# Two counts of a routing block in one PSUM bank

## The chip, the core and the metric

The kernel runs on one core of a Trainium2 chip. A core has a matrix engine (TensorE, PE in the profile; its weight loads are shown apart as PEld), a vector engine (VectorE, DVE), a scalar engine (ScalarE, ACT), a general engine (GpSimd, POOL) and a queue that mostly starts DMA transfers (SyncE, SP). Each engine takes its instructions in the order in which the program was built, and waits at an instruction until what it needs is there. Matrix products land in PSUM, which has eight banks of 2 KB per partition, 512 fp32 numbers each. The metric is the time of one execution on the device in microseconds, lower is better.

## What is computed

There are 8192 tokens of width 512. Each is normalised (layernorm); the result is the token plus an attention by random features plus a mixture of 64 experts plus a shared expert. Cut to what matters here:

```python
xn = _layernorm(x, axis=-1)
# attention: features of the tokens times features of the weights
feats = 1 / sqrt(512) * AB * exp(xn @ (ab[:, None] * proj).T - 0.5 * sum(xn * xn) * ab * ab)
attn = feats @ weights.T
# routing
scores = sigmoid(tokens @ router_w)                    # 64 experts
# the 4 best of 8 groups of experts, then the 8 best experts in them
topk_w, topk_idx = top_k(masked_scores, 8)
topk_w = topk_w / sum(topk_w) * 2.5
pos = number of earlier (token, slot) pairs that chose the same expert   # cumsum of a one-hot
valid = pos < 256                                      # capacity of an expert
# each expert: its tokens, silu(g) * u, down; added back with its weight
# shared expert: silu(tokens @ sg) * (tokens @ su) @ sd
out = x + attn + routed + shared
```

For the capacity the kernel has to know, per expert, how many tokens chose it up to each token. Those running counts are what the change touches.

## The kernel before, in words

The tokens are cut into 16 blocks of 512 (NB, TB), and each block into four parts of 128 tokens (NS). Products with fp32 accuracy are made of three matmuls on rounded upper parts and remainders (`products`, L108). The routing logits have such parts too, but the router's two parts lie side by side in one weight tile, so eight matmuls of 512 columns make them (L364).

The first stage, about the first 405 us, goes over the blocks with two strands. `dense` does an even block's shared expert (tiles ps_gu, then ps_o) and its attention features (ps_f, L501 to L507) and output (ps_o, L511). `routing(step)` is called after every step of `dense` and moves the routing of the blocks on by one step each; five steps make a block (GAP), so two blocks are routed while one even block is worked through densely. The features and outputs of most odd blocks are done later, in pieces between the experts' work. In the second stage the experts follow one another, each with two gathers of its rows by POOL, gate, up and down products, and a scatter that adds to the output.

The steps of one block's routing are the generator `look_up(b)`:

- `normalize`, ahead of it, writes the normalised tokens xw by ScalarE (L301). From block 5 on a DMA started by ScalarE copies them to a tile xc (L314), so that they can be read in another number type.
- `turn` transposes the block on TensorE into four PSUM tiles ps_x (L331), taken in turn from the pools `ps_tr` and `ps_sm`; ScalarE (L98) and VectorE (L101) split each into xT_h and xT_l.
- The logits: eight matmuls into ps_l (L364), copied by ScalarE to lt (L374).
- Four transposes bring lt back into token order, ps_lt (L381); ScalarE copies one half (L388), VectorE adds the other (L389), ScalarE writes exponentials into xw (L391).
- VectorE ranks the groups and takes the best eight (L397 to L426), makes the mask of chosen experts mask_r (L428) and prior_r, the number of earlier choices in the same partition (L435).
- One idle step. In it the next block's `turn` is issued, because the next block starts five steps after this one.
- The counts: one matmul of 256 columns into ps_b (L443), the counts before each part, and four of 128 columns into ps_u (L454), the running counts. ScalarE copies ps_u to cu (L462), which a DMA writes to the table upto in device memory (L463).
- In the next step VectorE reads ps_b twice to update the tables begun (L482), which later tell where each expert's tokens begin.

The blocks are called in order, so in one routing step the counts of block b come first and the logits of block b + 1 second; one step later begun of block b comes first and ps_lt of block b + 1 second.

PSUM is divided by pools: two banks for `ps_tr`, four for `ps_mm` (all products of `dense`), two for `ps_sm`:

```python
ps_tr = ctx.enter_context(tc.tile_pool(name="ps_tr", bufs=2, space=PSUM))
ps_mm = ctx.enter_context(tc.tile_pool(name="ps_mm", bufs=4, space=PSUM))
ps_sm = ctx.enter_context(tc.tile_pool(name="ps_sm", bufs=2, space=PSUM))
```

Half of the transposes, ps_l, ps_lt, ps_b and ps_u all share the two banks of `ps_sm`. Which tile gets which bank, and in what order an engine's instructions stand, is decided by a scheduler as the program is built. It keeps the given priorities, lets an instruction go ahead when it thinks its bank and operands are free, and adds the waits that order the engines, for each bank of PSUM too. `behind(a, b)` only adds that a stands behind b. So a change of the tiles can change the order of instructions, even though none is added.

Of the kernel before, what the change touches and what calls it, by code (L numbers as in the profile page):

```python
# [9 lines left out]
FP = mybir.dt.float32  # L10
# [8 lines left out]
P = 128  # L19
# [3 lines left out]
E = 64  # L23
# [8 lines left out]
TB = 512  # L32
NB = T // TB
NS = TB // P
# [19 lines left out]
def rfs_attention_moe_kernel(  # L54
# [22 lines left out]
    ps_sm = ctx.enter_context(tc.tile_pool(name="ps_sm", bufs=2, space=PSUM))  # L77
# [39 lines left out]
    def behind(a, b):  # L117

        tc.add_manual_dep(a.ins, b.ins.name, ORDER, reason="what a needs comes late")
# [223 lines left out]
    def look_up(b):  # L343
# [90 lines left out]
        for s in range(1, NS):  # L434
# [4 lines left out]
        yield  # L439
        yield  # L440

        pb = ps_sm.tile([P, NS, E], FP, tag="sm", name="ps_b")
        counted = nc.tensor.matmul(  # L443
            pb.rearrange("p s e -> p (s e)"),
            ones_r,
            prior_r.rearrange("p s e -> p (s e)"),
            start=True,
            stop=True,
        )
        behind(counted, last["pe"])  # L450
        pu = ps_sm.tile([P, NS // 2, P], FP, tag="sm", name="ps_u")
        for q in range(NS // 2):
            for part, (w, v) in enumerate(((mask_r, tri_r), (prior_r, ones_r))):
                nc.tensor.matmul(  # L454
# [197 lines left out]
    for rc in range(RC):  # L652
        pool, tag = ((ps_sm, "sm"), (ps_tr, "tr"))[rc // 2]
        ps_w.append(pool.tile([P, H], FP, tag=tag, name="ps_f"))
        projected(parts(wT, KC), rc, ps_w[rc])
    late = look_up(0)
    next(late)
    upper0 = last["upper"]
# [182 lines left out]
    def routing(t):  # L841

        for b in sorted(fronts):
            if next(fronts[b], fronts) is fronts:
                del fronts[b]
        b, k = divmod(t + GAP, GAP)
        if k == (b == 1) and b < NB:
            fronts[b] = look_up(b)
            next(fronts[b])
        if k == GAP - 3 and b + 1 < NB:  # L850
            normed[b + 1] = normalize(b + 1, *roots(b + 1, statistics(xbs[b + 1])))
        if k == 1 and b + 2 < NB:
            xbs[b + 2] = load_tokens(b + 2)
# [141 lines left out]
```

## Time and profile before

| what | value |
|---|---|
| three runs | 1320.38 us median (1320.17 to 1323.96) |
| the profiled execution | 1324.84 us, its span on the core 1323.1 us |
| granted TensorE clock | 0.998 |
| stage to 390 us: TensorE busy | 78.65 of 85.00 us, then 297.24 of 305.00 us |
| 390 to 445 us, where the experts begin | 51.68 of 55.00 us |
| 445 us to the end | 872.46 of 878.10 us |
| one count matmul, 256 columns, of ps_b | 0.28 us, the next starts 0.12 us later |
| one copy cu of ps_u by ScalarE | 0.37 us, 16 of them |
| one begun by VectorE | 0.48 us, 32 of them |
| one matmul of 512 columns | 0.39 us, the next starts 0.23 us later |

A row of the profile names the source line, engine and operation, the tile written and those read, the shapes and how many there are. A row of the timeline begins with the start and the time it took, and in brackets stands how long the engine was idle before it and what it waited for. Matmuls overlap, so a matmul's own time is longer than the distance between two starts. All is one execution.

### The profile page before, as it was taken

The numbers are of one execution on the slowest core, as the hardware profiler recorded it, in microseconds if no ns is written. First come the engines' busy times: TensorE is split into PE (matmuls) and PEld (weight loads), VectorE is DVE, ScalarE is ACT, GpSimd is POOL, SyncE is SP. The second block draws the span as 40 slices with busy tenths as digits, with TensorE's granted clock in tenths as the row PEclk, the third lists the DMA queues.
The fourth block names the chain that finished last, engine by engine and source line by source line (L and its number), as shares of the span: only waits on it lengthen the run. The fifth ranks groups of instructions, "written<-read, shape, count | busy, mean of one in ns | idle before, by whom it ended". The sixth has DMA issues, their size and how long they took to land.

```text
span 1323.1 us, 21351 instructions
## 1 busy us (share of the span) xinstructions
PE 1300.0 (98%) x7648; PEld 1138.6 (86%) x7648; DVE 929.2 (70%) x1922; ACT 646.1 (49%) x1017; POOL 573.1 (43%) x670
## 2 busy tenths in 40 slices
PE   8999999999999999999999999999999999999998
PEld 6888787788788899999999999999999999988886
DVE  7978768768765677777677767777776776643555
ACT  5644443444332455656556556655565565540111
POOL 3122012012105667778667676767677754210000
PEclk9999999999999999999999999999999999999999
DMA  7665675675585989999999999999999999875995
GB/s 253 239 229 198 234 259 197 233 266 209 193 314 178 305 216 306 270 276 271 317 271 264 309 265 283 248 294 285 266 259 303 281 259 234 227 220 178 317 319 191
DMA packets 192313, 338.60 MB, mean 256 GB/s; under 512 B 15952, under 2 KB 87632, under 8 KB 192208
## 3 DMA queue, kind: packets, MB, share of 16 engines
q1 hardware_dynamic: 153456, 245.93, 54.1%
q0 software_dynamic: 32768, 79.78, 27.3%
q10 hardware_dynamic: 5984, 11.54, 2.5%
q8 instruction: 60, 0.98, 0.3%
q14 instruction: 45, 0.37, 0.1%
HBM read 220.66 MB, written 104.99 MB: 246 GB/s over the span
## 4 chain that ended last, share of the span: by engine, by line
PE 90%; DVE 4%; DMA 4%; ACT 1%; issue 1%; POOL 0%; SPq 0%; DVEq 0%; ACTq 0%
PE ps_gu L108 41%; PE ps_o L108 14%; PE ps_e L108 13%; PE ps_fu L108 6%; PE ps_y L108 5%; PE ps_f L108 3%; PE ps_t L769 3%; DMA xc<-xw 2%; PE ps_l L364 2%; PE ps_x L331 2%; DMA xb<-in_L_attn_x_dram 1%; DVE f L491 0%; DVE r L499 0%; DVE fT L101 0%; DVE st L275 0%
## 5 line engine op out<-in xcount | busy, mean ns | idle before, releaser
L819 POOL DMA_INDIRECT out_dram<-ye,who x128 | 225.5, 1762 | 186.5 <-ACT ye L818 136.4
L108 PE MATMUL ps_gu<-gT,gu_h 128*128 128x256 f32 x2048 | 291.3, 284 | 0.0
L108 PEld LDWEIGHTS ps_gu<-gT,gu_h 128*128 128x128 f32 x2048 | 268.6, 192 | 5.3 <-ACT gu_h L98 1.0
L699 POOL DMA_INDIRECT at<-upto,line x128 | 140.2, 1095 | 80.1 <-DMA q<-norms 41.4
L108 PE MATMUL ps_gu<-gT,gu_l 128*128 128x256 f32 x1024 | 167.3, 286 | 0.2 <-DVE gu_l L101 0.2
L101 DVE TENSOR_TENSOR gu_l<-gu,gu_h 128x1024 fp32r<-128x1024 f32 x128 | 155.6, 1218 | 6.9 <-ACT gu_h L98 6.9
L752 POOL DMA_INDIRECT xg<-xnw,who x128 | 143.1, 1118 | 39.0 <-issue 32.6
L108 PE MATMUL ps_e<-d_h,ehT 128*128 128x512 f32 x512 | 148.6, 392 | 0.0
L108 PEld LDWEIGHTS ps_gu<-gT,gu_l 128*128 128x128 f32 x1024 | 140.9, 192 | 0.7 <-DVE gu_l L101 0.4
L98 ACT CAST gu_h<-gu 128x1024 fp32r<-128x1024 f32 x128 | 132.5, 1058 | 0.0
L246 POOL TENSOR_TENSOR a<-rstd,ve 128x4 f32<-128x4 f32 x45 | 10.5, 233 | 272.0 <-DVE rstd L242 269.6
L98 ACT CAST ehT<-sg 128x512 fp32r<-128x512 f32 x64 | 39.8, 621 | 156.6 <-DVE sg L499 153.7
L818 ACT ACTIVATE ye<-ps_e,we 128x512 f32<-128x512 f32 x128 | 88.6, 695 | 56.4 <-PE ps_e L108 55.6
L108 PEld LDWEIGHTS ps_e<-d_h,ehT 128*128 128x128 f32 x512 | 94.7, 188 | 18.8
L499 DVE SCALAR_TENSOR_TENSOR sg<-sg,ps_gu 128x512 f32<-128x512 f32 x64 | 44.0, 688 | 68.4 <-PE ps_gu L108 68.2
L101 DVE TENSOR_TENSOR d_l<-d,d_h 128x1024 fp32r<-128x1024 f32 x64 | 78.3, 1224 | 7.6 <-ACT d_h L98 7.2
L101 DVE TENSOR_TENSOR gT<-ps_t,gT 128x512 fp32r<-128x512 f32 x128 | 83.2, 682 | 0.0
L101 DVE TENSOR_TENSOR ehT<-sg,ehT 128x512 fp32r<-128x512 f32 x64 | 44.4, 694 | 51.8 <-ACT ehT L98 51.8
L505 ACT ACTIVATE f<-f,ab 128x512 f32<-128x512 f32 x64 | 46.4, 725 | 69.3 <-DVE f L491 69.3
L108 PE MATMUL ps_o<-fW_h,fT 128*128 128x512 f32 x288 | 79.3, 392 | 0.2 <-ACT fT L98 0.2
L108 PE MATMUL ps_e<-d_l,ehT 128*128 128x512 f32 x256 | 79.4, 391 | 0.0
L108 PE MATMUL ps_o<-d_h,hT 128*128 128x512 f32 x256 | 78.3, 396 | 0.0
(180 smaller groups left out, 2513.6 us busy)
## 6 DMA issues: line engine op xcount, KB each, us to landing
gu<-in_L_ffn_gate_w_dram SPq DMA_DIRECT2D x64, 512.0 KB
gu<-in_L_ffn_up_w_dram SPq DMA_DIRECT2D x64, 512.0 KB
d<-in_L_ffn_down_w_dram SPq DMA_DIRECT2D x64, 512.0 KB
xnw<-xw SPq DMA_DIRECT2D x32, 577.0 KB
xb<-in_L_attn_x_dram SPq DMA_DIRECT2D x32, 512.0 KB
out_dram<-xb SPq DMA_DIRECT2D x32, 512.0 KB
xT_h<-turned SPq DMA_DIRECT2D x30, 512.0 KB
xT_l<-turned SPq DMA_DIRECT2D x30, 512.0 KB
```

What stands on the lines that cost most here:

```text
L98: return nc.scalar.copy(dst, src)
L101: return on.tensor_tensor(dst, src, hi.bitcast(FP), ALU.subtract)
L108: last["pe"] = nc.tensor.matmul(ps, w[c][a], v[c][b], start=(start and part == 0 and c == 0), stop=(stop and part == 2 and c == n - 1),)
L331: last["turn"] = nc.tensor.transpose(pr[:, ts(s, P)], src(s)[:, ts(kc, P)], ident if dt is FP else ident_r)
L364: logits = nc.tensor.matmul(pl, rwp[:, kc].rearrange("p t e -> p (t e)"), v[kc], start=(n == 0 and kc == 0), stop=(n == 1 and kc == KC - 1),)
L499: nc.vector.scalar_tensor_tensor(dst, dst, 0.5, u, ALU.mult, ALU.mult)
L505: nc.scalar.activation(f, f, AF.Exp, scale=ab[:, rc : rc + 1])
L699: nc.gpsimd.indirect_dma_start(out=at[:, e % TE, h, :], out_offset=None, in_=upto, in_offset=bass.IndirectOffsetOnAxis(ap=line[:, e, h : h ...
L752: nc.gpsimd.indirect_dma_start(out=xgs[e][:, h, :], out_offset=None, in_=xnw, in_offset=bass.IndirectOffsetOnAxis(ap=who[:, e, h : h + 1], ...
L769: turned_s = nc.tensor.transpose(pr[:, c, ts(h, P)], xr[:, h, ts(c2 * 2 + c, P)], ident_r)
L818: nc.scalar.activation(ye[:, h, :], po, AF.Copy, scale=wes[e][:, h : h + 1])
L819: now = nc.gpsimd.indirect_dma_start(out=out, out_offset=bass.IndirectOffsetOnAxis(ap=who[:, e, h : h + 1], axis=0), in_=ye[:, h, :], in_o ...
```

## The change

The tiles ps_b and ps_u, which had a bank each, become the two halves of one tile ps_bu. The shapes and contents of the five count matmuls are as before, and so are the copies and the tables. The pool keeps its two banks.

```diff
@@ look_up @@
         yield
         yield
 
-        pb = ps_sm.tile([P, NS, E], FP, tag="sm", name="ps_b")
+
+        both = ps_sm.tile([P, 2, TB // 2], FP, tag="sm", name="ps_bu")
+        pb = both[:, 0].rearrange("p (s e) -> p s e", e=E)
         counted = nc.tensor.matmul(
-            pb.rearrange("p s e -> p (s e)"),
+            both[:, 0],
             ones_r,
             prior_r.rearrange("p s e -> p (s e)"),
             start=True,
             stop=True,
         )
         behind(counted, last["pe"])
-        pu = ps_sm.tile([P, NS // 2, P], FP, tag="sm", name="ps_u")
+        pu = both[:, 1].rearrange("p (q t) -> p q t", t=P)
         for q in range(NS // 2):
```

The lines behind it stand two lines lower in the changed kernel.

## The prediction

> **What bounds the kernel now.** I read the page's totals and its chain first, then the waits of TensorE, then the timeline around the instructions that the diff touches.
>
> ```profile
> span 1323.1 us, 21351 instructions
> PE 1300.0 (98%) x7648; PEld 1138.6 (86%) x7648; DVE 929.2 (70%) x1922; ACT 646.1 (49%) x1017; POOL 573.1 (43%) x670
> ...
> PE 90%; DVE 4%; DMA 4%; ACT 1%; issue 1%; POOL 0%; SPq 0%; DVEq 0%; ACTq 0%
> ```
>
> TensorE is busy 98% of the span, and 90% of the chain that ended last runs on it. So only what changes TensorE's own order or its pauses can move the end, and microsecond for microsecond, unless a later wait takes it back. Next, all waits of the logits matmuls (L364, tile ps_l), the instructions that are to get another bank:
>
> ```profile
> PE ps_l L364 <- ACT cu L462: 1.5, 7, 0.2
> PE ps_l L364 <- DVE xw L471: 1.2, 5, 0.2
> PEld ps_l L364 <- ACT cu L462: 4.5, 7, 0.6
> PEld ps_l L364 <- issue: 3.2, 5, 0.6
> ```
>
> Seven blocks' logits wait for ScalarE's copy cu (L462), five for something on VectorE. The timeline shows both kinds. First a block whose counts fall at the start of the features (columns: start, time, engine, line, what, how many, and the idle time before):
>
> ```profile
> 136.97 1.14 PE L108 MATMUL ps_f<-xT_h,pT_h 128*128 128x512 f32 x4
> 137.26 0.87 DVE L482 SCALAR_TENSOR_TENSOR begun<-ps_b,slot,begun 128x256 f32<-128x256 f32 x2
> 137.37 0.62 ACT L98 CAST hT<-r 128x512 fp32r<-128x512 f32 x1 [1.02 <-DVE r L499]
> 137.90 0.37 ACT L462 COPY cu<-ps_u 128x256 f32<-128x256 f32 x1
> 138.05 0.68 DVE L101 TENSOR_TENSOR hT<-r,hT 128x512 fp32r<-128x512 f32 x1
> ...
> 138.32 1.21 PE L364 MATMUL ps_l<-xT_h,rwp 128*128 128x512 f32 x4 [0.22 <-ACT cu L462]
> ...
> ```
>
> The logits start when cu, which had to follow the cast of hT on ScalarE, has emptied ps_u at 138.27. They need that bank. Then one in the middle of the output matmuls:
>
> ```profile
> 160.13 0.48 DVE L482 SCALAR_TENSOR_TENSOR begun<-ps_b,slot,begun 128x256 f32<-128x256 f32 x1 [0.53 <-PE ps_b L443]
> ...
> 160.32 0.68 PE L108 MATMUL ps_o<-fW_l,fT 128*128 128x512 f32 x2
> 160.53 0.37 ACT L462 COPY cu<-ps_u 128x256 f32<-128x256 f32 x1 [4.39 <-PE ps_u L454]
> 160.53 0.17 DVE L469 TENSOR_REDUCE den<-top 128x4 f32<-128x32 f32 x1
> 160.63 0.47 DVE L482 SCALAR_TENSOR_TENSOR begun<-ps_b,slot,begun 128x256 f32<-128x256 f32 x1
> ...
> 161.25 1.16 PE L364 MATMUL ps_l<-xT_h,rwp 128*128 128x512 f32 x4 [0.24 <-DVE xw L471]
> 162.25 1.08 PE L364 MATMUL ps_l<-xT_l,rwp 128*128 128x512 f32 x4
> ```
>
> Here the bank is that of ps_b. Its second reader begun ends at 161.10, and the logits follow. (The row names xw, L471, because that ended last before them; in the built program the logits read nothing of xw, and the bank's reader is begun.)
>
> **What the stalls cost now.** Here the idle column and the spacing disagree. The idle column gives TensorE 1.5 + 1.2 = 2.7 us. [...] By the busy rows the change could give 2.7 us at most (0.2%); by the spacing of starts it is more than twice that. I take the spacing, since starts are recorded and ends are modelled. Undisturbed, four matmuls of 512 columns take 0.91 us (the four at 141.21 are followed at 142.12), 0.227 each. Behind the small count matmuls the second matmul comes 0.06 late in every block; that stays.
> - Feature kind: four matmuls from 136.97 would let the logits start at 136.97 + 0.91 + 0.06 = 137.94; they start at 138.32: 0.38 lost. The first four logits then take 139.37 - 138.32 = 1.05 where 0.93 is usual for the second four (0.92): the restart costs 0.12. Sum 0.50, seven times: 3.5 us.
> - Output kind: two from 160.32 would end at 160.32 + 0.46 + 0.06 = 160.84; start 161.25: 0.41 lost, and 1.00 for the first four: 0.08. Sum 0.49, five times: 2.4 us.
> Together 5.9 us. A sixth block of the output kind (logits at 112.74) has no stall, and blocks 0 to 2 have their logits ahead of any count.
>
> **The change part by part.**
> - *Count matmuls.* The same five per block, same shapes, half a bank each: nothing added or removed on TensorE.
> - *Order on TensorE.* In the built program the eight logits matmuls stand directly behind the five counts in 13 blocks, ahead of the two to four ps_f or ps_o matmuls that stood between. Their bank is now the one that the transposes of the same block (ps_x) left; its readers, the xT_l subtractions, ended at 158.00 in the output kind, where the counts run from 159.81, and several us before in the other. So I expect no wait: minus 5.9 us. A satisfied wait still shows a hiccup: at 67.39 four logits with satisfied waits take 0.98 where 0.93 is usual. I charge 0.05 in 7 blocks, 0.35 us; the bounds are 0 and, if each restart cost stayed whole, 7 x 0.12 + 5 x 0.08 = 1.2.
> - *Block 2.* Here the logits stand before the counts, and the transposes ps_lt (L381) move up to directly behind the counts, from behind six matmuls. They need lt (L374), copied from 69.49 to 70.08. The counts begin at 69.29 and take 0.52, so TensorE is ready at 69.85 and waits to about 70.13: plus 0.28 us, once. In block 1 lt ends at 48.30, before the counts: nothing.
> - *begun behind cu.* [...] At 160.53 and 137.90 cu and begun do overlap now, from two banks. In the built program begun now waits for ScalarE. [...] By the rows I charge 0: in the new order VectorE first does work that is due anyway. Output kind: from 159.60, two statistics (0.66 each), an aggregate (0.17), den (0.17), two xw (0.23): to about 161.4, later than 160.90; then both begun, to about 162.2. Feature kind: the hT subtraction first (138.05 to 138.73), begun to about 139.6, in a stretch where VectorE then idles until 142.32. Behind begun on VectorE stand the block statistics, the next prior_r, and in the feature kind the exponent of the first ps_f, not due before 141.6.
> - *ps_lt behind begun.* The transposes take over the shared bank, so they wait for begun. Output kind: counts end at 160.37, logits at 162.2, then seven matmuls of 0.227: ps_lt is due at 163.8, cover 1.6 us over 162.2. Feature kind: due at 142.12 - 0.5 = 141.6 against 139.6, cover 2.0. lt is copied some 1 us earlier than now.
> - *One reordering on ScalarE.* In the first block that has xc, the first normalisation (L301) now stands ahead of the two exponentials xw (L391), and both transfers of xc behind all four normalisations. The first of these waits for POOL's shift and runs only at 120.36, so the exponentials slip by 3 us, for which nothing waits but the store of that block five steps later. But the first xc transfer goes from 121.91 to about 124, and the second from 124.20 to about 124.6. Now both have landed when the transposes begin at 129.56. The transposes at 151.92 began 6.3 us after the issue of 145.58: by that, data at about 130.9 for a TensorE that is due at about 129.3. Between 0 and 1.6 us, once; I take 0.4, since the transfer of 124.20 needed less than 5.4.
> - *SP and POOL.* POOL's order is unchanged; on SP one transfer of a norms row trades places in one early block. In the last block begun waits for cu, 402.35 in place of 402.08. That makes the row numbers for the searches 0.3 us later, but POOL starts them only at 405.25, 1.5 us after the row numbers (403.73): hidden, 0.3 at most.
>
> Sum: -5.9 + 0.35 + 0.28 + 0.4 = -4.9 us. The profiled execution would go from 1324.84 to about 1319.9; the median of the runs is 1320.38, 4.5 below it, and a stall of fixed length is worth the same there: **1315.5 us**, 0.4% less.
>
> **Rivals.**
> - *The gain is taken back at the next DMA wait.* Five blocks of the feature kind are followed by transposes that wait for xc (0.8 to 1.6 us; 0.89 idle shown at 151.92). If xc landed at a fixed time, the 0.5 us won before it would be waited there: five times, 2.5 us, end 1318.0. Against it: xc's second transfer is issued on ScalarE at 145.58, behind the features' exponentials (143.10) that TensorE feeds, so it should move with TensorE.
> - *The stalls stay.* If what held the logits were VectorE's xw or TensorE's switch between groups, nothing would go: about 1320. The row naming xw speaks for it, cu's end 0.05 before the logits in the feature kind against.
> - *Slower: begun comes too late for ps_lt.* TensorE waits in order, so everything behind it is late. Cover is 1.6 to 2.0 us; it breaks even at 4.9 / 13 = 0.4 us beyond it, when begun ends some 2.2 us later than I work out, because cu waits for ScalarE or VectorE's queue slips. At 3 us late: 13 x 1.2 = 15.6, end 1320.4 - 4.9 + 15.6 = 1331.1. Against it: ScalarE was idle 4.39 us before cu in one kind, and cu ends at 138.27 in the other.
>
> **How the numbers follow.** About 0.3% (4.0 us) is what can be told from no change here. Stalls gone and kept: 0.62, at 1315.5, own range 1313.4 to 1316.9; some 0.03 of it lies above 1316.4. Taken back in part: 0.17, near 1318.0. Stalls stay: 0.12, near 1320. Slower: 0.09. Upper end of the gain: 5.9, the 0.06 behind the counts in 13 blocks (0.8), and a shorter xc wait in one block (0.8): 7.5, low end 1312.8. High end 1320.8 takes in the second and third cases. Faster by over 0.3% (below 1316.4): 0.59; within: 0.32; slower: 0.09.
>
> **What would show it.** TensorE's waits have no row of ps_l on cu, nor on VectorE or "issue" in more than the first blocks; the logits start within 0.2 us of the last count; the first four take 0.93 to 0.98. A new row of ps_lt waiting for lt, 0.2 to 0.3 us, once. begun starts after cu's end in every block and no ps_lt waits for begun. The five xc waits, 5.0 us on TensorE, stay as they are, and one may be added at about 129. The prediction is wrong if ps_lt waits for begun in many blocks, if the xc waits grow by 0.5 each, or if the logits still start late.

## The result and the profile after

The changed kernel takes 1315.44 us (median of 20 runs, 1313.67 to 1321.07), the kernel before beside it 1320.41 us (20 runs, 1318.99 to 1326.92). The ratio is 0.9964, 95% interval 0.9952 to 0.9975: 5.0 us, or 0.4%, less. The profiled execution went from 1324.84 us to 1314.5 us; that pair of executions differs by twice as much as the medians do, and the text below says where the rest lies. First the page of the changed kernel, its totals and its chain:

```profile
span 1312.8 us, 21348 instructions
PE 1295.3 (99%) x7648; PEld 1138.5 (87%) x7648; DVE 929.3 (71%) x1922; ACT 645.9 (49%) x1017; POOL 568.3 (43%) x670
...
PE 86%; DMA 5%; DVE 4%; ACT 1%; POOL 1%; issue 1%; SPq 1%; DVEq 0%; ACTq 0%
```

TensorE bounds the kernel as before: it issues the same 7648 matmuls and is busy 99% of a shorter span. Then the waits of TensorE that the profile lists for the changed kernel (engine, tile and line, what it waited for: us in all, times, the longest):

```profile
PE ps_x L331 <- DMA wi<-_attn_input_weights_dram: 4.9, 3, 3.6
PE ps_x L331 <- DMA xc<-xw: 4.4, 5, 1.1
PE ps_fu L108 <- DVE yb L596: 1.0, 1, 1.0
PE ps_lt L381 <- ACT lt L374: 0.9, 2, 0.7
PE ps_gu L108 <- DVE xT_l L101: 0.2, 1, 0.2
PE ps_o L108 <- ACT fT L98: 0.2, 1, 0.2
```

The twelve waits of the logits ps_l for cu and for VectorE (listed as xw) are gone. The five waits for xc are still there, and ps_lt waits for lt twice. Now the timeline around a block whose counts fall at the start of the features, the one that was shown from 136.97 (columns as there):

```profile
136.80 0.28 PE L456 MATMUL ps_bu<-ones_r,prior_r 128*128 128x128 f32 x1
...
136.91 1.15 PE L364 MATMUL ps_l<-xT_h,rwp 128*128 128x512 f32 x4
...
137.85 0.37 ACT L464 COPY cu<-ps_bu 128x256 f32<-128x256 f32 x1
137.90 1.08 PE L364 MATMUL ps_l<-xT_l,rwp 128*128 128x512 f32 x4
...
138.59 0.87 DVE L484 SCALAR_TENSOR_TENSOR begun<-ps_bu,slot,begun 128x256 f32<-128x256 f32 x2
...
138.81 1.09 PE L108 MATMUL ps_f<-xT_h,pT_h 128*128 128x512 f32 x4
```

The logits start 0.11 us after the last count's start, and the first four take 137.90 - 136.91 = 0.99. The features follow them; cu and begun run while TensorE is already elsewhere. The output kind, shown before from 160.13:

```profile
159.46 0.28 PE L456 MATMUL ps_bu<-ones_r,prior_r 128*128 128x128 f32 x1
...
159.57 1.15 PE L364 MATMUL ps_l<-xT_h,rwp 128*128 128x512 f32 x4
159.77 0.37 ACT L464 COPY cu<-ps_bu 128x256 f32<-128x256 f32 x1 [4.41 <-PE ps_bu L456]
160.06 0.23 DVE L473 TENSOR_SCALAR xw<-den 128x2 f32<-128x2 f32 x2
...
160.19 0.87 DVE L484 SCALAR_TENSOR_TENSOR begun<-ps_bu,slot,begun 128x256 f32<-128x256 f32 x2
...
160.56 1.08 PE L364 MATMUL ps_l<-xT_l,rwp 128*128 128x512 f32 x4
```

The same picture: nothing between counts and logits. All 13 blocks that have their logits behind the counts look like one of these two. What that is worth can be read from starts alone. From the first count to the first matmul behind a block's counts, products and logits, the same 17 matmuls of a feature block took 3.82 to 3.84 us and now take 3.34; the 15 of an output block took 3.35 to 3.36 (2.95 in the one without a stall) and now take 2.88 (2.93). Over the 13 blocks 46.5 us have become 40.7.

**Where the 10.3 us of the profiled pair went.** The first count of the last block starts at 401.27 us before and at 395.25 us after: 6.0 us are won by then. The other 4.3 us lie where the experts begin. Three windows of the kernel before show it (start and end, length, then busy us and number of TensorE matmuls, weight loads, VectorE, ScalarE and GpSimd, then the granted TensorE clock, the DMA share and GB/s):

```profile
438.00:439.20 1.20, 0.59 (x3) 0.50 (x4) 1.20 (x4) 0.00 (x0) 0.90 (x1) 1.00 1.08 351
439.20:442.60 3.40, 3.40 (x19) 3.40 (x18) 1.62 (x7) 0.00 (x0) 2.79 (x3) 0.52 0.92 310
442.60:446.00 3.40, 3.40 (x30) 3.40 (x30) 0.64 (x1) 0.60 (x1) 2.48 (x4) 0.98 0.94 243
```

Before, TensorE waited 2.8 us for yb, into the first of these windows, and then had 3.4 us at about half the clock (0.52). After, the wait for yb is 1.0 us and the clock from 390 to 445 us is 1.00. The shorter wait is 1.8 us, and 3.4 us at half the clock cost at most 1.7; the last 0.8 us were not traced. Other executions have such pauses of other lengths at this place (3.6 us in a second trace of the kernel before, 5.8 and 4.4 in two of the changed kernel, each with time at half the clock), so this part can't be put down to the change. It also fits the times: the profiled execution before lay 4.4 us above its kernel's median, the one after 0.9 us below.

### The profile page after: what moved, and what is told of

It reads as the page before. It is cut to its first block, busy times and chain, and to the rows that moved or that the text cites. A ratio compares the mean times of both kernels' runs of the same rounds, so it can differ in the third digit from the quotient of the medians.

```text
span 1312.8 us, 21348 instructions
## 1 busy us (share of the span) xinstructions
PE 1295.3 (99%) x7648; PEld 1138.5 (87%) x7648; DVE 929.3 (71%) x1922; ACT 645.9 (49%) x1017; POOL 568.3 (43%) x670
## 4 chain that ended last, share of the span: by engine, by line
PE 86%; DMA 5%; DVE 4%; ACT 1%; POOL 1%; issue 1%; SPq 1%; DVEq 0%; ACTq 0%
PE ps_gu L108 41%; PE ps_e L108 13%; PE ps_o L108 13%; PE ps_y L108 5%; PE ps_fu L108 5%; PE ps_t L771 3%; DMA xc<-xw 2%; PE ps_f L108 2%; PE ps_x L331 2%; PE ps_l L364 1%; DMA xb<-in_L_attn_x_dram 1%; DMA at<-upto,line 1%; POOL at L701 1%; DVE st L275 1%; DVE fT L101 0%
```

## The experiments

The chips of the experiments gave the kernel before 1334 to 1336 us, at a granted clock near 0.995 where the first pair had 0.998 and 0.999. The first stage is not what takes longer there: the last block's counts begin at 401.07 us in the repeat, at 401.27 in the first trace. The repeat is 9.0 us behind by the 400th of the experts' gate and up matmuls (542.3 against 533.3), and 8.9 at the end. So each run is compared as a ratio with the kernel before on its own chip, and 0.996 stands for the gain of the change.

**The two kernels again.** The kernel before once (1333.78 us), the changed kernel on the same chip:

> The kernel before, unchanged, for a second trace of it. Theory (the stalls are built into the order of the program): the same twelve stalls of ps_l, 2.7 us in the idle column, the last block's counts at about 401 us. Rival (what was read from one execution was chance): other blocks, or sums that differ by more than 1 us.

> The changed kernel, unchanged, to stand beside the next two. Theory: ratio 0.995 to 0.998, the last block's counts 5 to 7 us earlier than in the kernel before, no wait of ps_l for cu, xw or issue. Rival: a part of the gain in the profile came from chance, the counts less than 4 us earlier.

The ratio is 0.9959 (0.9945 to 0.9972), and the last counts begin at 395.72 us, 5.35 us earlier. On another chip:

> The changed kernel once more, beside the kernel before, so that the next run has it on the same chip. If the gain is the removed stalls, the ratio is again 0.9955 to 0.9972 and no logits wait for cu.

The ratio is 0.9967 (0.9955 to 0.9979). With the first result, three measurements agree on 0.996 to 0.997. The kernel before shows its two waits again, with the same numbers:

```profile
PE ps_l L364 <- ACT cu L462: 1.5, 7, 0.2
PE ps_l L364 <- DVE xw L471: 1.2, 5, 0.2
```

and the changed kernel has neither. By starts, the 13 blocks again take 46.5 us in the one and 40.7 in the other.

**Only the logits get another bank.** The counts keep one bank each, the logits move to the pool of the transposes:

```diff
-        pl = ps_sm.tile([P, TB], FP, tag="sm", name="ps_l")
+        pl = ps_tr.tile([P, TB], FP, tag="tr", name="ps_l")
```

> The kernel before with one edit: the logits tile ps_l comes from the pool ps_tr, the two counts keep a bank each. Theory (the logits waited for a bank that the counts' readers still held): the logits no longer wait for cu or begun, all 5.9 us of stalls go, about 1315 us as in the changed kernel, ratio near 0.996. Rival (sharing one bank, or the new order behind it, is what gains): about 1320, ratio 1.000.

The ratio is 0.9967 (0.9956 to 0.9979), as with the change. No logits wait for cu or VectorE, and the last counts begin at 395.8 us, where the kernel before has 401.1 in its repeat. So sharing a bank between the counts is not needed for the gain: another bank for the logits does it too. (TensorE's order moved here as well: in seven blocks the logits stand directly behind the counts, in six others ahead of them. The next experiment parts bank and order. The profiled execution of this kernel was the longest of its seven, 1336.97 against a median of 1331.15 us; it has a pause of 13.6 us where the experts begin.)

**The shared bank with the old order.** Beside the bank, the change moved the logits ahead of two to four products. Here they are held behind them again, in the changed kernel, from block 3 on:

```diff
+HELD = {1: 4, 0: 13}
...
+                if "held" in last:
+                    last["left"] -= 1
+                    if not last["left"]:
+                        behind(last.pop("held"), last["pe"])
...
                     behind(logits, last["pe"])
+                    if b > 2:
+                        last["held"], last["left"] = logits, HELD[b % 2]
```

> The changed kernel, with the logits held behind the same two to four ps_f or ps_o matmuls as in the kernel before (from block 3 on), so that the bank is new and TensorE's order old. Theory (bank): no wait of ps_l for cu or begun, about 1315.5 us, ratio 0.996 to 0.997. Rival (the order: logits earlier, so that what follows them is earlier): the gain is lost, 1319 to 1320.

The ratio is 0.9972 (0.9956 to 0.9989); the interval overlaps that of the change. The timeline of TensorE in a block of the feature kind:

```profile
137.56 0.28 PE L463 MATMUL ps_bu<-ones_r,prior_r 128*128 128x128 f32 x1
137.67 1.14 PE L109 MATMUL ps_f<-xT_h,pT_h 128*128 128x512 f32 x4
138.65 1.08 PE L369 MATMUL ps_l<-xT_h,rwp 128*128 128x512 f32 x4
139.56 1.08 PE L369 MATMUL ps_l<-xT_l,rwp 128*128 128x512 f32 x4
140.48 1.09 PE L109 MATMUL ps_f<-xT_l,pT_h 128*128 128x512 f32 x4
```

The order is that of the kernel before, and the logits start 0.98 behind the features' start, without a stall, and their first four take 0.91. The 13 blocks take 40.5 us, as against 40.7 with the new order. So the gain is the bank's, and the new order adds nothing to it that these runs can tell.

**The old banks with the new order.** Now the other half alone: two banks for the counts as before, and a product is held behind the logits. In the seven feature blocks this puts the logits directly behind the counts, as meant. In the output blocks it does not: three products still stand between, where the kernel before has two or three.

```diff
+HELD = {1: 1, 0: 12}
...
+                if "held" in last:
+                    last["left"] -= 1
+                    if not last["left"]:
+                        behind(last["pe"], last.pop("held"))
...
                     behind(logits, last["pe"])
+                    if b > 2:
+                        last["held"], last["left"] = logits, HELD[b % 2]
```

> The kernel before, with the logits forced directly behind the counts, so that the order is about the new one and the banks are the old ones. Theory (bank): the two to four matmuls that covered the wait are gone; the logits wait for a count's reader for about 1.2 us in 7 blocks of the feature kind (now 0.4) and 0.6 in 6 of the output kind (now 0.4): some 6 us slower than before, about 1326. Rival (order): about 1315, as the changed kernel.

The ratio is 1.0111 (1.0097 to 1.0126): 1349.16 us against 1334.56, 14.6 us more. A block of the feature kind (TensorE alone):

```profile
138.29 0.28 PE L461 MATMUL ps_u<-ones_r,prior_r 128*128 128x128 f32 x1
139.75 1.20 PE L369 MATMUL ps_l<-xT_h,rwp 128*128 128x512 f32 x4 [1.19 <-ACT cu L469]
140.79 1.08 PE L369 MATMUL ps_l<-xT_l,rwp 128*128 128x512 f32 x4
```

Now the logits stand directly behind the counts, in the bank that cu has to empty, and start 1.46 us behind the last count where the changed kernel needs 0.11. It happens seven times. In the output kind no logits wait, so the new order was tried with the old banks in the feature kind only. Its waits:

```profile
PE ps_l L369 <- ACT cu L469: 8.3, 7, 1.2
PE ps_x L336 <- DMA xc<-xw: 8.3, 4, 3.1
```

The 17 matmuls of a feature block take 4.75 us in place of 3.82, seven times; the 15 of an output block take 2.88 in place of 3.36, five times. Together that is 4.1 us more. The rest is a chain behind the stalls. The waits for xc are 8.3 us in place of 3.9 in the repeat of the kernel before, two of them 3.1 and 2.9 us long: the xc transfer that was issued at 146.50 and was there at 152.7 in that repeat is issued at 147.91 and is there at 156.4 here. Why it took 2.3 us longer was not tried; the DMA share from 145 to 153 us is 0.95 to 0.98 in both. And each of the two long pauses is followed by a lower clock. Around the first:

```profile
152.00:155.00 3.00, 1.36 (x8) 0.97 (x6) 2.95 (x7) 0.69 (x2) 0.00 (x0) 1.00 1.04 381
155.00:162.00 7.00, 5.56 (x23) 4.79 (x24) 4.46 (x21) 3.31 (x7) 0.00 (x0) 0.53 0.08 30
162.00:170.00 8.00, 8.00 (x38) 6.53 (x38) 5.13 (x23) 0.90 (x2) 0.41 (x3) 0.98 0.21 75
```

The granted clock is 0.53 in the seven us from 155, and again half for 3.4 us from 261. Ten us at half the clock cost at most five. By the last counts this execution is 11.9 us behind the repeat of the kernel before (412.95 against 401.07): 4.1 from the blocks, 4.4 from the waits for xc, and 3.4 left, which the lower clock can account for. At the end it is 11.6 us behind. The medians differ by 14.6, since the profiled execution was the fastest of its four; what the others lose beyond it was not traced. The expectation was missed on the size, because it counted only the stalls themselves, and took it that the output kind would stall too.

**A third bank for the small tiles.** If what is missing is banks, one could be taken from the products of `dense`:

```diff
-    ps_mm = ctx.enter_context(tc.tile_pool(name="ps_mm", bufs=4, space=PSUM))
-    ps_sm = ctx.enter_context(tc.tile_pool(name="ps_sm", bufs=2, space=PSUM))
+    ps_mm = ctx.enter_context(tc.tile_pool(name="ps_mm", bufs=3, space=PSUM))
+    ps_sm = ctx.enter_context(tc.tile_pool(name="ps_sm", bufs=3, space=PSUM))
```

> The kernel before, with three banks for ps_sm and three for ps_mm in place of two and four: the counts and the logits have a bank each, and the dense and expert products one bank fewer. Theory (the logits need any free bank): the waits of ps_l on cu and begun go, 5.9 us; against that stands what the products lose with three banks: the experts' gate, up and down tiles take turns in them, and each of the 64 experts may wait for an evacuation of 0.6 to 0.7 us once or twice, up to 50 us; I expect 1330 to 1350, slower than before. Rival (a bank too few in ps_mm costs nothing, its evacuation is always hidden): about 1315.

The ratio is 1.0005 (0.999 to 1.002), no difference. The logits no longer wait for cu, but the start pays for it:

```profile
0.00:85.00 85.00, 74.38 (x349) 60.72 (x350) 71.10 (x213) 42.46 (x76) 19.38 (x82) 0.98 0.63 213
85.00:390.00 305.00, 300.24 (x1499) 250.81 (x1498) 227.27 (x738) 134.16 (x255) 45.35 (x204) 1.00 0.65 236
...
470.00:1160.00 690.00, 690.00 (x4696) 634.16 (x4695) 501.47 (x754) 413.02 (x599) 458.41 (x342) 1.00 0.98 270
```

From 85 to 390 us TensorE is busy 300.24 us, against 298.36 in the repeat of the kernel before; in the first 85 us it is busy 74.38 against 78.16, with one pause of 4.3 us of ps_f and 3.4 us at half the clock behind it. The third block's counts begin 6.5 us later than in that repeat (96.2 against 89.7), the last block's 1.7 later. The experts are as full with three banks as with four, 690.00 of 690 against 689.87. The slowdown that was expected did not come: what three banks cost lies in the start, and the logits that wait no more pay for it. So a bank for the logits is no gain where the tiles that give it up then wait for it.

**The waits for xc, taken away too.** In the changed kernel the transfers of xc stand on ScalarE's queue. GpSimd has little to do in that stage (41.64 us of 305), so it starts them:

```diff
-                nc.scalar.dma_start(t, w[:, :, :H])
+                nc.gpsimd.dma_start(t, w[:, :, :H])
```

> The changed kernel, with the transfers of xc started by POOL's queue in place of ScalarE's. The prediction said that they are paced by ScalarE's order behind TensorE (issued at 143.86 and 145.58 though their source is written at 136.35). If so they start up to 7 us sooner in the feature kind, the five waits of ps_x on xc (some 5 us on TensorE) go, and the time is about 1311, 4 to 5 us below the changed kernel. Rival (the transfers are bound by the DMA engines, or POOL's queue starts them no sooner): no change, 1315 to 1316.

The ratio is 0.9945 (0.9932 to 0.9958). Since that interval overlaps those of the changed kernel, it was run again beside it on one chip:

> The changed kernel with both xc transfers started by GpSimd, once more. If the waits for xc are a second cost of their own, which comes on top of the stalls of the logits, this is 0.1 to 0.4% under the changed kernel of the same chip, that is a ratio of 0.992 to 0.9955. If what they cost is waited for again where the experts begin, as with the logits in ps_tr and the transfers on GpSimd, the ratio is 0.996 to 1.000.

1327.22 us (five runs, 1327.09 to 1328.82) against 1331.20 for the changed kernel (six runs, 1330.10 to 1332.55), the kernel before 1336.01: ratios 0.9942 (0.9928 to 0.9956) and 0.9967 (0.9955 to 0.9979). Every run of this version lies below every run of the changed kernel, by 4.0 us in the medians. For the transposes at about 151 us, the second transfer leaves at 137.54 us, right behind its source, where in the changed kernel it leaves at 144.83, and the last counts begin at 392.31 in place of 396.29. In its list of TensorE's waits the row of xc is gone:

```profile
PE ps_x L331 <- DMA wi<-_attn_input_weights_dram: 5.6, 3, 3.6
...
PE ps_lt L381 <- ACT lt L374: 0.6, 2, 0.4
PE ps_bu L445 <- DVE prior_r L435: 0.2, 1, 0.2
```

where the changed kernel of that chip has

```profile
PE ps_x L331 <- DMA xc<-xw: 5.6, 5, 1.2
```

5.6 us of waits gave 4.0. A new, small one has come in: the counts now reach their place before prior_r is ready.

**Both together on the old counts.** The logits in the transposes' pool (first experiment) with xc started by GpSimd:

> The kernel before with two edits: the logits in ps_tr (the two counts keep their banks), and the transfers of xc started by POOL. Theory (the two waits are independent): the sum of what each gave, ratio 0.9967 - 0.0019 = 0.995, and no wait of ps_l or ps_x on either. Rival (the one only uncovers the other, or a wait of the counts for VectorE): 0.997.

The ratio is 1.0002 (0.9993 to 1.0011): no gain at all, though the last counts begin at 394.1 us, 7.0 us before those of the kernel before on that chip. No logits wait; of the waits for xc one of 1.3 us is left, and the counts wait for prior_r three times, 0.8 us in all. The gain is given back where the experts begin (the waits there, all engines):

```profile
PE ps_y L108 <- DVE yb L594: 18.2, 1, 18.2
POOL xg L752 <- issue: 17.7, 10, 15.0
DVE yb L594 <- remote: 13.4, 1, 13.4
```

TensorE waits 18.2 us for one copy yb of VectorE, and VectorE waits before that copy 13.4 us for something that the profile names only as remote. The clock is 0.50 from 428 to 445 us. The logits' bank won alone, the xc transfers won on top of the shared bank (on the kernel before they were not tried alone), and together they gave nothing here. Why VectorE stands still there is open. Neither trace of the first pair has such a wait. In the repeat of the kernel before VectorE waits for remote 4.5 us in that place (and ScalarE 10.2), in the first experiment 21.0 us, in the first run of the changed kernel with xc by GpSimd 14.2 us before yb, in one profiled execution each. The last two kernels kept a gain, 0.9967 and 0.9945, so such a wait alone doesn't tell that the gain is lost. No run tells whether the pools' order or a late load of something is behind it. It does show that the place at 420 to 450 us can take back a gain of the first stage.

## Why the prediction was right

Forecast 1315.5 us, measured 1315.44. By its steps, in the profiled executions, with starts compared as the prediction did:

- *The stalls of ps_l, -5.9.* Right. Read by starts, the 13 blocks became 5.8 us shorter, in the first pair and in the two repeats on one chip. The choice between the idle column (2.7 us) and the spacing of starts (5.9 us) decided the forecast, and this settles it; the kernel whose logits have another bank agrees, with last counts 5.3 us earlier than those of the kernel before in its repeat.
- *+0.35 left over.* Not needed. The first four logits do take 0.98 to 0.99, some 0.05 over the usual, but this is the late second matmul behind the small counts (0.286 us between the first two starts, where 0.23 is usual). It fell on the features or outputs before, and the prediction counted it apart, as what stays. With the shared bank and the old order it is back on the features, whose four take 0.98, and the logits' first four take 0.91.
- *begun behind cu, 0.* Right: in the built program begun stands behind cu, and that cost nothing here. Before, the two ran at the same time (begun from 160.13 to 161.10, cu from 160.53 to 160.90). The group of begun in the changed kernel:

```profile
L484 DVE SCALAR_TENSOR_TENSOR begun<-ps_bu,slot,begun x32: 472/478/484, 56.2 to 396.8; 128x256 f32<-128x256 f32 x32
its engine sat idle before it (us, times) until:
  ACT cu L464: 0.2, 1
who waited for it (us, times):
```

  VectorE waited for cu once in 32, 0.2 us. If the order alone had moved it from 160.13 to cu's end at 160.90, and as far in each of the 13 blocks, that would have been 13 x 0.77, some 10 us (an estimate from the rows before). The order is kept: in all 16 blocks begun starts after cu's end. In the output kind cu ends at 159.77 + 0.37 = 160.14 and begun starts at 160.19. VectorE did other work in between.
- *ps_lt behind begun.* Right. The last line of the group has nothing under it: nobody waited for begun. In the output kind both begun end at about 160.19 + 0.87 = 161.06, and ps_lt starts at 163.09, 2.0 us later (1.6 was forecast); in the feature kind at 139.46 and 141.56, 2.1 us (2.0).
- *Block 2's ps_lt waits for lt, +0.28.* Right, with 0.33 by starts. (The prediction's own figures give 0.32: 69.29 + 0.52 is 69.81, not 69.85.)

```profile
69.79 0.59 ACT L374 COPY lt<-ps_l 128x512 f32<-128x512 f32 x1 [2.73 <-PE ps_l L364]
...
70.42 0.42 PEld L381 LDWEIGHTS ps_lt<-ident,lt 128*128 128x128 f32 x4 [0.30 <-ACT lt L374]
```

- *The second wait of ps_lt is not the change's.* In block 0 the logits wait 0.28 us for an early step of VectorE in the first trace of the kernel before, and ps_lt 0.26 for lt; in the changed kernel the logits don't wait and ps_lt waits 0.71. In the repeats it is the other way round: the kernel before has the one wait, 0.75, the changed kernel the two, 0.28 and 0.24. So this differs from execution to execution, and is worth 0.1 us.
- *ScalarE's reordering, +0.4.* Wrong, and it cost nothing. The step said that both transfers of xc would stand behind all four normalisations and leave at about 124 and 124.6. They left at 122.34 and 123.75, and the transposes at 129.5 wait for nothing. All five waits for xc together are 0.6 us shorter in this pair (5.0 and 4.4), 0.4 longer in the repeats (3.9 and 4.3), and 5.6 in the third trace of the changed kernel: no effect of the change that these traces can tell.

The sum in the profiled pair: -5.8 (stalls) + 0.33 (ps_lt of block 2) - 0.1 (block 0) - 0.6 (xc) = -6.2, where -6.0 is read from the last counts; the repeats have -5.35 there. The forecast was -4.9, because it charged 0.35 and 0.4 that did not come. And what arrives at the end is less sure than that sum: the medians differ by 5.0, 5.6 and 4.8 us in the three comparisons of the two kernels. The mechanism and the size were right; that the forecast met the median within 0.1 us is luck, inside its own range of 1313.4 to 1316.9.

Of the rivals, "the gain is taken back at the next DMA wait" fell with the waits for xc, which did not grow by 0.5 each; "the stalls stay" fell with the list of waits; "slower" with the empty line under begun. What no rival had is the place where the experts begin. There the profiled pair won 4.3 us more, and one experiment lost all that it had won.

## What to carry to other kernels

When an engine in order waits for a PSUM bank, look for the readers of the tile that had the bank last, and for any spare half of a bank: tiles that are written together and read by engines that have other work in between can share one, and the freed bank was worth the whole stall here, 5.8 us over 13 blocks. Price a stall by the spacing of starts, with the slow restart (0.12 us in the feature kind, 0.08 in the output kind), not by the idle column, and check the order in which the readers of the shared bank then stand. And read on to the next stage: here a gain of 5 to 7 us arrived at the end in most versions and in one not at all, and behind pauses of 2.8 to 3.1 us TensorE had another 3.4 us and more at about half the clock.

## What was not expected of the hardware

Time at half the granted clock stood behind stretches in which TensorE did little. Between the first record of the clock and the last matmuls the kernel before has it once, for 3.41 us. A cut into stretches of that length shows the pause of 2.8 us, the half clock and what follows (columns as above):

```profile
435.90:439.31 3.41, 0.70 (x4) 0.61 (x5) 3.41 (x7) 0.72 (x2) 2.80 (x3) 1.00 1.05 381
439.31:442.72 3.41, 3.41 (x19) 3.41 (x18) 1.51 (x5) 0.00 (x0) 2.73 (x3) 0.50 0.93 312
442.72:446.14 3.42, 3.42 (x30) 3.42 (x30) 0.69 (x1) 0.60 (x1) 2.58 (x3) 1.00 0.94 238
```

TensorE was busy for 0.70 of 3.41 us, and the next 3.41 us ran at 0.50. The five waits for xc in the same trace, up to 1.5 us long, left the clock at 1.00 (85 to 390 us). Two stretches with the old banks and the new order differ too:

```profile
206.65:210.06 3.41, 2.32 (x21) 2.00 (x20) 2.95 (x8) 1.29 (x4) 0.00 (x0) 1.00 0.85 327
210.06:213.47 3.41, 3.41 (x17) 2.80 (x16) 3.41 (x19) 2.04 (x5) 0.00 (x0) 1.00 0.00 0
257.85:261.26 3.41, 1.60 (x16) 1.56 (x17) 1.14 (x3) 1.19 (x3) 0.00 (x0) 1.00 0.28 109
261.26:264.68 3.42, 3.42 (x10) 2.65 (x9) 3.42 (x18) 2.11 (x6) 0.00 (x0) 0.50 0.00 0
```

Behind the one that was busy for 2.32 of 3.41 us the clock was 1.00, behind the one with 1.60 it was 0.50. With three banks each TensorE was busy for 0.89 of the 5 us from 15 us; the clock was 0.64 in the four us from 20, and 1.00 in the four behind them. In the third trace of the changed kernel a pause of 4.43 us ends at 423.90; the clock was 0.50 from 425.0 to 428.4, 0.83 in the next 3.4 us, and 1.00 from 431.8. What decides when it falls and when it comes back was not shown. The program's first matmuls ran slowly too: the kernel before starts its transposes 0.21 us apart up to 9.2 us, where the record of the clock begins, and 0.11 apart behind it.

So a wait could cost more than its length here: in the kernel before, the 3.41 us at half the clock behind the 2.8 us cost up to 1.7 more, half of 3.41 (an estimate).
